# A MetaFormer layer on one core: the spectral products at full width with zero blocks instead of quarter-array products

## The chip, the core and the metric

The kernel runs on one core of a Trainium2 chip. The core has a matrix engine (TensorE, PE in the profile; its weight loads are listed as PEld), a vector engine (VectorE, DVE), a scalar engine (ScalarE, ACT), GpSimd (POOL) and a queue engine (SyncE, SP). Matmuls read SBUF and write PSUM, whose banks hold 512 float32 columns in each of 128 partitions. Each engine works through its own instructions in order; semaphores tie them together. The metric is device time in microseconds (us) of one execution; lower is better.

## The reference

One layer over x of shape (8, 128, 128, 96): a spectral mixer with a residual, then a quantised FFN with a residual.

```python
# x: (8, 128, 128, 96); MED = 192
x_pre = _soa(jnp.einsum('bhwc,mc->bhwm', _ln_c(x), w1), soa1_scale, soa1_bias)   # scale * relu(.)^2 + bias
xf = rfft2(x_pre over h, w)                                  # 128 x 65 complex, per channel
...
r = softmax over 3 of an MLP of (mean of x, mean of relu(bn(x @ sp_w)))           # (B, 3, 192)
comb = jnp.einsum('shwm,bsm->bhwm', filt, r)                 # filt: three small kernels, resized by matrices
xsp = irfft2(xf * comb)
x = x + jnp.einsum('bhwm,cm->bhwc', xsp, w2)
...
t = t + _ffn_ref(_ln_t(t), W1, b1, W2, b2)                   # fp8 (5, 2) products, 96 -> 384 -> 96
```

Both Fourier transforms are done as matrix products. All of the mixer is float32; the FFN's products are fp8.

## The kernel before

Each of the eight batches passes through three streams of operations, called `a`, `s` and `c`.

Stream `a` (32 units of four columns w): load and normalise x, project it to 192 channels plus 48 for the context (`project`, L881), rectify and square on ACT, transform along h (`transform`, L910), fold the two halves of w on DVE and store Y to DRAM. At its end the `rate_*` steps make the softmax weights `rates[b]`, one row of 2 x 192 values per partition.

Stream `s` works on groups `g` of two frequency rows h, 33 groups a batch. `load_y` brings the group's Y: 128 partitions are 64 folded positions i = 0 and 64 of i = 1, and for each there are four rows (cosine and sine of two frequencies, index `2 * cs + k`) of 192 channels. `load_t` and `weigh` (POOL) bring and scale the filter coefficients. Then, on PE,

- `along_w` (L1104) transforms along w. It cuts the 192 channels in three thirds `q` of 64. Each product is 64 rows deep (i), 64 channels wide (the half k of the output partitions) and 65 columns long; 24 a group, each on its own quarter of the array.
- `filters_of` (L1119) spreads the filter coefficients to 65 frequencies: 6 products 64 rows deep (s), 128 channels wide (two rows of one third) and 130 columns long, two halves of the array at a time.
- after `copy_sr` (ACT), `make`, `times` (DVE) and `turn_back` (POOL) have multiplied spectrum and filter into `xf`, `mix_low` and `mix` (L1200) multiply pairs `p` of groups by w2: 96 products a pair, 64 deep, 64 wide, 96 columns, accumulating over `q`, in two PSUM banks `pv`, one for each of the two frequency rows r.

`mixed` (ACT) copies half of the sums to `B`, `combine` (DVE) adds and subtracts, `invert` (L1241, L1243) transforms back along w, `inverted` (ACT) and `store_v` write V to DRAM.

Stream `c` (32 units a batch): load V and x, transform back along h (`last`, L1337), add the residual, normalise, quantise, transpose (`turn8`, L1366), first layer (`first`, L1384), cast, bias, relu on ACT and DVE, second layer (`second`, L1411), sum and store.

The order in which these operations are written to the engines is made in `in_order`: a list scheduler with a table `COST` (engine and us for each kind), a `WINDOWS` entry and an `OFFSETS` entry that give each operation its place in a priority line, and six PSUM banks to hand out. `QUARTER` names the kinds that use a divided array; a change between these and others has its own overlap in `MODES`, and `TURN` is a penalty in the priority. `WARM` names operations before which some matmuls of zeros are issued (`keep_warm`, L587). All engines then run in the written order.

Of the kernel before, what the change touches and what calls it, by code (L numbers as in the profile page):

```python
# [43 lines left out]
MED = 192  # L44
# [3 lines left out]
NS = 3  # L48
# [20 lines left out]
    "a": ((-1014.7, 224.2), (1155.2, 782.6), (913.1, 640.2), (700.4, 97.1), (81, 727.1), (986.1, 683.8), (1759.7, 398.2), (2087.9, 538.4)),  # L69
    "s": ((159.4, 351.5), (85.6, 1024.7), (720.2, 346.4), (408.4, 331.2), (-141.4, 469.9), (-95.4, 205.3), (797.8, 257), (1809.8, 30.5)),  # L70
    "c": ((1028.7, 511.2), (1109.6, 188.3), (1290.9, 349.7), (1829.7, 439.1), (2176.6, 456.9), (2490.5, 149.5), (2420.5, 484.7), (2163.8, 1143.1)),
}
OFFSETS = {
    "a_context": -69.32,
    "a_fold": 73.44,
    "a_inverse": -262.16,
    "a_load_r": 18.09,
    "a_load_x": 271.95,
    "a_load_xT": -31.56,
    "a_measure": 23.91,  # L80
    "a_project": 117.85,
    "a_put": 26.98,
    "a_rate_e": 26.43,
    "a_rate_n": 275.68,
    "a_rate_p0": -178.47,
    "a_rate_p1": 125.73,
    "a_rate_p2": -434.33,
    "a_rate_v0": -18.7,
    "a_rate_v1": 37.77,
    "a_rate_v2": 27.67,  # L90
    "a_rate_v3": 53.52,
    "a_rectify": -24.16,
    "a_rest": 88.21,
    "a_root": -155.19,
    "a_scale": 83.17,
    "a_square": 92.51,
    "a_store_r": 7.65,
    "a_store_y": -218.91,
    "a_transform": -124.2,
    "a_variance": -11.06,  # L100
    "c_accumulated": -194.42,
    "c_add_up": -37.31,
    "c_bias": -232.6,
    "c_biased": -34.16,
    "c_first": -3.46,
    "c_hidden": -99.06,
    "c_hidden_2": 18.08,
    "c_hidden_v": 120.54,
    "c_inverse": -69.89,
    "c_last": -164.57,  # L110
    "c_load_v": -0.91,
    "c_measure": 206.09,
    "c_put8": 55.17,
    "c_quantise": 161.11,
    "c_quantise_v": 272.29,
    "c_residual": -76.16,
    "c_rest": -195.99,
    "c_root": 122.09,
    "c_second": -129.32,
    "c_store": 584.16,  # L120
    "c_turn8": -377.8,
    "c_turned8": 104.13,
    "c_turned8_v": -71.45,
    "c_variance": -123.83,
    "s_alone_t": 236.02,
    "s_alone_x": 109.24,
    "s_alone_z": 223.71,
    "s_along_w": -28.38,
    "s_combine": -31.52,
    "s_copy_sr": 140.45,  # L130
    "s_filters_of": 27.98,
    "s_invert": 0.86,
    "s_inverted": -111.88,
    "s_load_t": 225.43,
    "s_load_y": 199.13,
    "s_make": 124.58,
    "s_mix": 88.61,
    "s_mix_low": -10.96,
    "s_mixed": -366.14,
    "s_store_v": 136.77,  # L140
    "s_times": -505.74,
    "s_turn_back": 28.39,
    "s_weigh": -53.57,
}
WAIT, PATIENCE, TURN = (0, 0, 0, 0.27, 0.89), (85, 74.3, 16.6, 0.273, 8.9), 454.49
# [3 lines left out]
    ('a', 0): {('project', 10, 0): 4, ('transform', 15, 2): 5, ('project', 17, 0): 4, ('project', 18, 0): 4, ('project', 19, 0): 4, ('project', 20, 0): 4, ('project', 21, 0): 4, ('project', 22, 0): 4, ('project', 23, 0): 4, ('project', 24, 0): 4, ('project', 25, 0): 4, ('project', 26, 0): 4, ('project', 27, 0): 4, ('project', 28, 0): 4, ('project', 29, 0): 4, ('project', 30, 0): 4, ('project', 31, 0): 4},  # L149
    ('a', 1): {('project', 0, 0): 4, ('transform', 0, 2): 7, ('transform', 1, 2): 4},  # L150
    ('c', 1): {('second', 12): 4, ('second', 18): 4},
    ('s', 2): {('along_w', 7): 4},
    ('a', 3): {('project', 6, 0): 3},
    ('c', 5): {('second', 21): 20, ('second', 29): 10},
    ('c', 6): {('second', 10): 12, ('second', 12): 4, ('second', 24): 14, ('second', 25): 10, ('first', 26, 0): 3, ('first', 28, 0): 4, ('first', 29, 0): 6, ('turn8', 7, 3): 10},
    ('s', 7): {('mix_low', 15): 7},
    ('c', 7): {('second', 1): 4, ('second', 5): 24, ('first', 6, 0): 8, ('second', 9): 5, ('second', 11): 9, ('last', 3, 0): 6, ('second', 13): 8, ('first', 15, 0): 4, ('second', 15): 14, ('first', 16, 0): 3, ('second', 17): 5, ('second', 19): 9, ('last', 5, 0): 16, ('second', 21): 7, ('turn8', 5, 3): 24, ('second', 23): 14, ('turn8', 6, 0): 24, ('first', 24, 0): 7, ('second', 24): 6, ('first', 25, 0): 4, ('second', 26): 8, ('second', 28): 12, ('second', 30): 10, ('turn8', 7, 3): 8, ('first', 31, 0): 4, ('second', 31): 6},
# [29 lines left out]
    "s_along_w": (PE, 0.88, 0),  # L187
    "s_filters_of": (PE, 0.94, 0),
# [4 lines left out]
    "s_weigh": (POOL, 1, 0),  # L193
    "s_mix_low": (PE, 1.22, 0),
    "s_mix": (PE, 1.22, 0),
    "s_mixed": (ACT, 0.325, 0),
    "s_combine": (DVE, 0.347, 0),
    "s_invert": (PE, 0.845, 0),
    "s_inverted": (ACT, 0.482, 0),
    "s_alone_z": (ACT, 0.75, 0),  # L200
    "s_alone_t": (DVE, 2.1, 0),
# [53 lines left out]
QUARTER = {"s_along_w", "s_filters_of", "s_mix_low", "s_mix"}  # L255
SHARED = {"a_scale", "c_biased", "a_rate_n", "a_rate_v3", "c_quantise_v", "c_hidden_v"}
INSTR = {
    "a_project": 8, "a_transform": 4, "a_rate_p0": 4, "a_rate_p1": 8, "a_rate_p2": 12, "s_along_w": 96,
    "s_filters_of": 24, "s_mix_low": 96, "s_mix": 96, "s_invert": 4, "c_last": 4, "c_turn8": 8, "c_turn32": 16,
# [33 lines left out]
def _columns(p, r):  # L293

    if p < NP - 1:
        return [(2 * p + i, k) for k in range(2) for i in range(2)]
    return [(NG - 1, 0), (NG, 0), (NG - 1, 1), (NG, 1), (NG + 1, 0)] if r == 0 else [(NG - 1, 0), (NG + 1, 0), (NG - 1, 1)]


def _constants():  # L300
# [22 lines left out]
    for p in range(NP):  # L323
        for cs in range(2):
            for r in range(2):
                for g in (2 * p, 2 * p + 1):
                    turned.append(g + 1 + 32 * r + 64 * cs if g < NG or r == 0 else 64 * (1 - cs))
    out = {
        "F1": np.concatenate([cos, sin[1:-1]])[rows].T * norm,
        "F2": np.concatenate([np.stack([half[0], -half[0]], 1), np.stack([half[1], half[1]], 1)]) * norm,  # L330
# [36 lines left out]
    rw[1, :, 1] *= -1  # L367
    out["RW"], out["SEL"] = rw.reshape(128, 2 * L), np.concatenate([sel, sel])
# [178 lines left out]
def metaformer_kernel(ctx: ExitStack, tc: tile.TileContext, a: dict, out: bass.AP):  # L547
# [68 lines left out]
    F2 = load(T_CONST, "F2", [128, 2, L])  # L616
    RW = load(T_CONST, "RW", [128, 2 * L])
    soa_bias = spread(T_CONST, "soa1_bias", 128)

    w2C = load(T_CONST, "w2C", [128, 3, C])  # L620
# [3 lines left out]
    w2N = const.tile([128, 3, C], F32, name="w2N")  # L624
# [6 lines left out]
    def projection(sp):  # L631
# [35 lines left out]
        def others():  # L667
            nc.vector.tensor_scalar(w2N, w2C, -1.0, None, ALU.mult)
            make_identity(nc, ident)
            nc.vector.tensor_copy(ident8, ident, saturate=False)  # L670
            nc.vector.memset(ones, 1.0 / (H * W))
            nc.vector.tensor_scalar(soa_bias, soa_bias, 128.0, None, ALU.mult)
# [5 lines left out]
        at(T_CONST, others, after=[(None, "soa1_bias"), (None, "w2C")])  # L678
# [155 lines left out]
    def before(b, t0, P):  # L834
# [155 lines left out]
        def rate_v2():  # L990
            hr = pa.tile([RHID, 1], F32, name="hr", tag="hr")
            hm = pa.tile([RHID, 1], F32, name="hm", tag="hm")
            kept["hrep"] = hrep = pa.tile([RHID, 128], F32, name="hrep", tag="hrep", bufs=1)
# [59 lines left out]
    def spectrum(b, t0, P):  # L1053
# [31 lines left out]
        def weigh(g):  # L1085
            p = slice(0, 128 if g <= NG else 64)
            tw = kept["tw", g] = psp.tile([128, 2 * MED], F32, name="tw", tag="tw", bufs=1)
            tb, order = kept.pop(("tb", g)), "p (k q m) -> p k q m"
            nc.gpsimd.tensor_tensor(  # L1089
                tw[p, :].rearrange("p (q k m) -> p k q m", q=3, k=2),  # L1090
                tb[p, :].rearrange(order, k=2, q=3),
                rates[b][p, :].rearrange(order, k=2, q=3),
                ALU.mult,
            )

        def along_w(g):
            halves = [bank("pz") for _ in range(2)]
            kept["pz", g] = halves
            for cs in range(2 if g <= NG else 1):
                for q in range(3):  # L1100
                    for k in range(2):
                        for i in range(2):
                            rows, c = slice(64 * i, 64 * i + 64), 2 * q + (cs if i == 0 else 1 - cs)
                            nc.tensor.matmul(  # L1104
                                halves[i][64 * k : 64 * k + 64, c * L : (c + 1) * L],
                                lhsT=kept["yt", g][rows, 2 * cs + k, 64 * q : 64 * q + 64],
                                rhs=F2[rows, cs, :],
                                start=True,
                                stop=True,
                            )  # L1110
# [26 lines left out]
        def make(g, i):  # L1137
            if ("d", g) not in kept:
                work("d", g, 2, 3, 2, L)
# [50 lines left out]
        def mix_part(p, columns):  # L1190

            for i in columns:
                for q in range(3):
                    for h in range(2):
                        for r in range(2):
                            if i >= len(_columns(p, r)):
                                continue
# [359 lines left out]
```

## Time and profile before

| | us |
|---|---|
| median of 3 runs | 2733.72 (2731.16 to 2736.47) |
| profiled execution, its own time | 2741.53 |
| its span in the profile | 2739.4 |
| PE busy | 2517.3 (92%) |
| DVE busy | 2280.6 (83%) |
| ACT busy | 2143.5 (78%) |
| POOL busy | 1691.3 (62%) |
| mean granted PE clock | 0.966 |

Busy is the time in which at least one instruction of an engine is under way. For matmuls it includes the pipeline's tail, so it overstates how full PE is. A line of the list of groups has the source line, engine, operation, output and inputs by their names in the program, the partitions x elements, the count, then the busy time, the mean length of one in ns, and the idle time before them with what ended it. One float32 product is two matmul records. HBM traffic is 407.03 MB read and 208.16 MB written, 225 GB/s over the span.

### The profile page before, as it was taken

To read this page: it belongs to the slowest core of one execution; us is meant where nothing else is said; L and a number is where in the kernel's file an instruction comes from. 1 tells how busy PE (TensorE), PEld (TensorE's weight loads), DVE (VectorE), ACT (ScalarE), POOL (GpSimd) and SP (SyncE) were. 2 spreads that over 40 slices of the span, in tenths; PEclk is the share of its full clock that TensorE was granted. 3 is DMA by queue.
4 is the path that set the end of the run, shared out by engine and by line. 5 is a ranking of instruction groups with operands and counts; after the bars stand their busy time and mean duration, and the time that the engine had idled before them with its cause. 6 is when DMAs were issued, how large, how long until landed. Compare 5 with 4: busy or idle time off the path is not lost.

```text
span 2739.4 us, 92861 instructions
## 1 busy us (share of the span) xinstructions
PE 2517.3 (92%) x37514; PEld 1803.0 (66%) x37514; DVE 2280.6 (83%) x5485; ACT 2143.5 (78%) x4332; POOL 1691.3 (62%) x2535
## 2 busy tenths in 40 slices
PE   7899999999899999899999999999999998999887
PEld 4557777767667776666776776766667665666444
DVE  5568697888898888978888988888979988889786
ACT  2356666649889798887998788988989888988866
POOL 3235454546576657756777576857766676788444
PEclk8899999999999999999999999999999999999889
DMA  8789899998867987587768988786768666575341
GB/s 227 243 262 302 255 279 291 285 272 276 260 192 244 291 258 204 186 259 240 231 198 258 289 257 260 224 243 199 234 190 250 192 201 187 153 230 157 107 137 46
DMA packets 506110, 621.22 MB, mean 227 GB/s; under 512 B 165197, under 2 KB 440038, under 8 KB 505658
## 3 DMA queue, kind: packets, MB, share of 16 engines
q1 hardware_dynamic: 417618, 464.28, 57.7%
q10 hardware_dynamic: 88064, 151.02, 15.5%
q8 instruction: 295, 4.83, 0.8%
q14 instruction: 133, 1.09, 0.1%
HBM read 407.03 MB, written 208.16 MB: 225 GB/s over the span
## 4 chain that ended last, share of the span: by engine, by line
PE 42%; ACT 17%; DVE 11%; issue 6%; DMA 4%; POOL 3%; ACTq 0%; SPq 0%; POOLq 0%; DVEq 0%
PE px L881 7%; PE py L910 6%; PE pv L1200 5%; ACT y L1391 4%; PE pf L1119 4%; PE pz L1104 4%; PE pg L1241 4%; PE pk L1337 4%; ACT h L1404 3%; ACT z L1361 3%; PE ph L1384 3%; PE po L1411 2%; DMA vin<-Vd 2%; DVE y L1395 2%; DVE t L1148 1%
## 5 line engine op out<-in xcount | busy, mean ns | idle before, releaser
L881 PE MATMUL px<-W1S,zT 97*128 97x240 f32 x2048 | 505.0, 381 | 10.6 <-DVE yst L922 5.5
L881 PEld LDWEIGHTS px<-W1S,zT 97*128 97x128 f32 x2048 | 393.1, 196 | 123.6 <-PE warm L587 10.4
L1089 POOL TENSOR_TENSOR tw<-tb,r 128x384 f32<-128x384 f32 (+1 forms) x264 | 292.1, 1106 | 259.2 <-PE pf L1119 127.6
L910 PE MATMUL py<-X,F 128*128 128x384 f32 x1024 | 435.3, 515 | 17.0 <-DVE t L1343 3.1
L1391 ACT CAST y<-ph 128x512 f16<-128x512 f32 x768 | 417.1, 604 | 25.6 <-PE ph L1384 21.6
L1404 ACT ACTIVATE h<-y 128x1536 fp8e5<-128x1536 f16 (+1 forms) x256 | 371.1, 1450 | 29.2 <-DVE y L1395 26.3
L892 ACT ACTIVATE rl<-px 128x480 f32<-128x480 f32 x512 | 292.7, 579 | 127.5 <-PE px L881 94.1
L1361 ACT ACTIVATE z<-t,ln_m,ln_r 128x96 fp8e5<-128x96 f32 x848 | 361.3, 475 | 9.1 <-POOL ln_m L826 5.6
L1395 DVE TENSOR_TENSOR y<-y,b1q 128x1536 f16<-128x1536 f16 x256 | 321.5, 1256 | 54.2 <-ACT y L1391 52.8
L906 POOL TENSOR_TENSOR sacc<-sacc,rl 128x192 f32<-128x192 f32 x248 | 175.1, 706 | 289.4 <-ACT rl L892 277.3
L1200 PE MATMUL pv<-w2C,xf 64*64 64x96 f32 x9264 | 315.6, 246 | 28.5 <-issue 25.4
L922 DVE TENSOR_TENSOR yst<-py,yb 128x384 f32<-128x384 f32 x512 | 261.7, 546 | 74.0 <-ACT rl L892 24.2
L1200 PEld LDWEIGHTS pv<-w2C,xf 64*64 64x64 f32 x9264 | 273.2, 134 | 62.7 <-issue 45.7
L1142 DVE TENSOR_TENSOR d<-pz,sr 128x390 f32<-128x390 f32 x512 | 265.2, 554 | 42.1 <-ACT sr L1135 41.7
L1148 DVE TENSOR_TENSOR t<-d,pf 128x780 f32<-128x780 f32 x256 | 245.3, 958 | 53.2 <-PE pf L1119 33.2
L1162 POOL TENSOR_TENSOR xf<-t 128x390 f32<-128x390 f32 x256 | 234.5, 916 | 66.6 <-DVE t L1148 57.6
L1119 PE MATMUL pf<-RW,tw 64*128 64x130 f32 x3120 | 252.4, 292 | 20.8 <-DVE t L1153 11.1
L1104 PE MATMUL pz<-F,yt 64*64 64x65 f32 x12480 | 250.0, 223 | 18.6 <-issue 13.2
L1384 PE MATMUL ph<-zT,W1q 96*128 96x512 fp8e5 x768 | 242.1, 387 | 23.3 <-ACT y L1391 6.5
L1426 POOL TENSOR_TENSOR o<-o,b2q 128x1536 f16<-128x1536 f16 x64 | 200.5, 3132 | 94.1 <-ACT o L1422 93.5
L1104 PEld LDWEIGHTS pz<-F,yt 64*64 64x64 f32 x12480 | 217.3, 136 | 61.4 <-issue 26.9
L1119 PEld LDWEIGHTS pf<-RW,tw 64*128 64x128 f32 x3120 | 201.3, 189 | 82.8 <-issue 30.2
(132 smaller groups left out, 5129.7 us busy)
## 6 DMA issues: line engine op xcount, KB each, us to landing
Yd<-yst ACTq DMA_DIRECT2D x256, 384.0 KB
yt<-Yd SPq DMA_DIRECT2D x248, 384.0 KB
xb<-in_xw SPq DMA_DIRECT2D x64, 768.0 KB
zT<-in_xT SPq DMA_DIRECT2D x128, 384.0 KB
rB<-Rd SPq DMA_DIRECT2D x128, 384.0 KB
tb<-T SPq DMA_DIRECT2D x256, 192.0 KB
Vd<-gst ACTq DMA_DIRECT2D x128, 384.0 KB
t<-in_x SPq DMA_DIRECT2D x64, 768.0 KB
```

The costliest lines, as they stand in the source:

```text
L881: nc.tensor.matmul(px[:, i * (MED + SCTX) : (i + 1) * (MED + SCTX)], lhsT=zTs[(b * NU // 2 + u // 2) % NZT][:, QW * (u % 2) + i0 + i, :], ...
L892: nc.scalar.activation(kept["rl", u][:, i0 : i0 + 2, :].rearrange("h w m -> h (w m)"), kept.pop(("px", u, i0)), AF.Relu)
L910: nc.tensor.matmul(py, lhsT=F1, rhs=kept["X", u][:, i0 : i0 + 2, :].rearrange("h w m -> h (w m)"), start=True, stop=True)
L1089: nc.gpsimd.tensor_tensor(tw[p, :].rearrange("p (q k m) -> p k q m", q=3, k=2), tb[p, :].rearrange(order, k=2, q=3), rates[b][p, :].rearra ...
L1104: nc.tensor.matmul(halves[i][64 * k : 64 * k + 64, c * L : (c + 1) * L], lhsT=kept["yt", g][rows, 2 * cs + k, 64 * q : 64 * q + 64], rhs=F ...
L1119: nc.tensor.matmul(pf[:, s, q * 2 * L : (q + 1) * 2 * L], lhsT=tw[p, 128 * q : 128 * q + 128], rhs=RW[p, :], start=True, stop=True,)
L1200: nc.tensor.matmul(kept["pv", p, r][half, i * C : (i + 1) * C], lhsT=kept["xf", g][rows, k, q, half], rhs=(w2N if k == 1 and h == 1 else w ...
L1361: nc.scalar.activation(z, t, AF.Identity, bias=m, scale=r, saturate=False)
L1384: nc.tensor.matmul(kept["ph", u, n], lhsT=W1q[:, n * 128 : (n + 1) * 128], rhs=kept["zT", u], start=True, stop=True)
L1391: nc.scalar.copy(kept["y", u][:, n, :], kept.pop(("ph", u, n)))
L1395: nc.vector.tensor_tensor(y, y, b1q, ALU.add)
L1404: nc.scalar.activation(h, y, AF.Relu, saturate=False)
```

## The change

The 192 channels of the two rows `k` of a group are read as one run of 384 and cut into three units of 128: the first row's channels 0 to 127, then its last 64 and the second row's first 64, then the second row's channels 64 to 191. Every product of the three lines then uses 128 rows and 128 channels, and the matrices carry zeros where a half must not contribute: F2 (transform along w) has the cosine columns in rows 0 to 63 and the sine columns in rows 64 to 127; RW (filters) has one block of 130 columns for each half; w2Z holds w2 for the shared unit, padded with zeros for each row. A group's transform has 6 products of 130 columns, its filters 4 (two of 260 columns, two of 130), a mixing part 3 for each group (192, 96 and 96 columns).

```diff
-QUARTER = {"s_along_w", "s_filters_of", "s_mix_low", "s_mix"}
+QUARTER = set()
...
-    "s_along_w": (PE, 0.88, 0),
-    "s_filters_of": (PE, 0.94, 0),
+    "s_along_w": (PE, 0.92, 0),
+    "s_filters_of": (PE, 0.84, 0),
...
-    "s_weigh": (POOL, 1, 0),
-    "s_mix_low": (PE, 1.22, 0),
-    "s_mix": (PE, 1.22, 0),
-    "s_mixed": (ACT, 0.325, 0),
-    "s_combine": (DVE, 0.347, 0),
+    "s_weigh": (POOL, 0.93, 0),
+    "s_mix_low": (PE, 0.98, 0),
+    "s_mix": (PE, 0.98, 0),
+    "s_mixed": (ACT, 0.485, 0),
+    "s_combine": (DVE, 0.552, 0),
...
+    f2 = np.zeros((128, 2, 2, L))
+    f2[:64, 0, 0], f2[64:, 0, 1], f2[:64, 1, 1], f2[64:, 1, 0] = half[0], -half[1], half[0], half[1]
...
+    signs = np.zeros((2, 64, 2, 2 * L))
+    for i in range(2):
+        signs[i, :, i] = rw[i].reshape(64, 2 * L)
+    out["RW"], out["SEL"] = signs.reshape(128, 4 * L), np.concatenate([sel, sel])
...
-            nc.gpsimd.tensor_tensor(
-                tw[p, :].rearrange("p (q k m) -> p k q m", q=3, k=2),
-                tb[p, :].rearrange(order, k=2, q=3),
-                rates[b][p, :].rearrange(order, k=2, q=3),
-                ALU.mult,
-            )
+            nc.gpsimd.tensor_tensor(tw[p, :], kept.pop(("tb", g))[p, :], rates[b][p, :], ALU.mult)
+
+        def unit(t, u):
+
+            return t.rearrange("p k m -> p (k m)")[:, 128 * u : 128 * u + 128]
 
         def along_w(g):
...
+            kept["pz", g] = [bank("pz") for _ in range(2 if g <= NG else 1)]
+            for cs in (1, 0) if g <= NG else (0,):
+                for u in range(3):
                     nc.tensor.matmul(
+                        kept["pz", g][cs][:, u * 2 * L : (u + 1) * 2 * L],
+                        lhsT=unit(kept["yt", g][:, 2 * cs : 2 * cs + 2, :], u),
+                        rhs=F2[:, cs, :],
                         start=True,
                         stop=True,
                     )
 
+        def filters_of(g):
+            pf = kept["pf", g] = psz.tile([128, 2, 512], F32, name="pf", tag="pf")
+            p = slice(0, 128 if g <= NG else 64)
+            tw = kept.pop(("tw", g))[p, :].rearrange("p (k m) -> p k m", k=2)
+            if g <= NG:
+                parts = ((0, 0, 0, 2), (1, 0, 2, 1), (1, 1, 0, 1), (2, 1, 1, 2))
+            else:
+                parts = ((0, 0, 0, 1), (1, 0, 1, 1), (2, 0, 2, 1))
+            for u, half, slot, n in parts:
+                s = 1 if (u, half) == (1, 1) else 0
+                nc.tensor.matmul(
+                    pf[:, half, slot * 2 * L : (slot + n) * 2 * L],
+                    lhsT=unit(tw, u),
+                    rhs=RW[p, s * 2 * L : (s + n) * 2 * L],
+                    start=True,
+                    stop=True,
+                )
...
-                work("d", g, 2, 3, 2, L)
+                work("d", g, 3, 2, 2 * L)
             op = ALU.subtract if i == 0 else ALU.add
-            d = kept["d", g][:, i].rearrange("p q c l -> p (q c l)")
-            nc.vector.tensor_tensor(d, kept["pz", g][0][:, : 6 * L], kept["sr", g], op)
+            a, b = (t.rearrange("p (u n) -> p u n", u=3) for t in (kept["pz", g][0][:, : 6 * L], kept["sr", g]))
+            nc.vector.tensor_tensor(kept["d", g][:, :, i, :], a, b, op)
...
+        def mix_part(p, s):
+
+            pv = kept["pv", p, s] = bank("pv")
+            for g in (2 * p, 2 * p + 1) + ((NG + 1,) if p == NP - 1 and s == 0 else ()):
+                x = kept["xf", g]
+                c0 = 2 * (g - 2 * p) - (g > NG)
+                rows = (0,) if g == NG else (0, 1)
+                nc.tensor.matmul(
+                    pv[:, c0 * C : (c0 + len(rows)) * C],
+                    lhsT=x[:, 2 + s, :],
+                    rhs=w2Z[:, rows[0] : rows[0] + len(rows), :].rearrange("m r c -> m (r c)"),
+                    start=True,
+                    stop=False,
+                )
+                for i, r in enumerate(rows):
+                    nc.tensor.matmul(
+                        pv[:, (c0 + i) * C : (c0 + i + 1) * C], lhsT=x[:, 4 * r + s, :], rhs=w2A[:, r, :], start=False, stop=r == rows[-1]
+                    )
 
         def mix_low(p):
...
+            mix_part(p, 1)
 
         def mix(p):
...
+            mix_part(p, 0)
+
+        def mixed(p):
+            v = kept["B", p] = psp.tile([128, 4 * C], F32, name="B", tag="B")
+            n = (3 if p == NP - 1 else 4) * C
+            nc.scalar.copy(v[:, :n], kept["pv", p, 1][:, :n])
...
+        def combine(p, cs):
...
+            at(t, mix_low, p, after=xf, banks=1, until=[one("mixed", p)])
+            at(t, mix, p, after=[one("mix_low", p)], banks=1, until=[done])
+            at(t + 0.0003, mixed, p, after=[one("mix_low", p)] + [one("combine", p - 2, cs) for cs in range(2)] + last)
+            for cs in range(2):
+                at(t + 0.1 * cs * P + 0.0004, combine, p, cs, after=[one("mix", p), one("mixed", p), v_free[cs]])
```

Left out above: the second mixing sums and the last group (`alone_*`) follow the same layout; `w2N`, the negated copy of w2, is gone; a small tile of the softmax steps (`hrep`) shares its buffer with another (`mx`). `mixed` copies all 384 columns of one bank at once, and `combine` runs twice a pair instead of four times. All values of `WINDOWS`, `OFFSETS`, `WAIT`, `PATIENCE` and `TURN` are others, so the written order of every engine is another. `WARM` issues 787 matmuls of zeros instead of 472. Behind the last mixing product PE has 180 first-layer products instead of 120.

## The prediction

> **What bounds the kernel now.** I read the busy shares first, then the slices, then TensorE's groups, then three stretches, then the order of single groups.
>
> ```profile
> span 2739.4 us, 92861 instructions
> PE 2517.3 (92%) x37514; PEld 1803.0 (66%) x37514; DVE 2280.6 (83%) x5485; ACT 2143.5 (78%) x4332; POOL 1691.3 (62%) x2535
> PE   7899999999899999899999999999999998999887
> PEclk8899999999999999999999999999999999999889
> ...
> L1200 PE MATMUL pv<-w2C,xf 64*64 64x96 f32 x9264 | 315.6, 246 | 28.5 <-issue 25.4
> L1119 PE MATMUL pf<-RW,tw 64*128 64x130 f32 x3120 | 252.4, 292 | 20.8 <-DVE t L1153 11.1
> L1104 PE MATMUL pz<-F,yt 64*64 64x65 f32 x12480 | 250.0, 223 | 18.6 <-issue 13.2
> ```
>
> PE is the fullest engine in nearly every slice, at a granted clock near 1, and the three lines that the change rewrites are among its largest. Each float32 product is two matmul records in the trace, two passes. A mean of 223 ns for a 65-column pass says little, because passes overlap; I need the time from the start of one group to the start of the next. That is in the order of PE's instructions (start, length, count):
>
> ```profile
> 1405.42 0.97 PE L881 MATMUL px<-W1S,zT 97*128 97x240 f32 x4
> 1406.23 0.39 PE L1366 MATMUL pz<-ident,z 128*96 128x128 fp8e5 x4
> 1406.46 0.81 PE L1384 MATMUL ph<-zT,W1q 96*128 96x512 fp8e5 x3
> 1407.11 0.97 PE L881 MATMUL px<-W1S,zT 97*128 97x240 f32 x4
> ...
> 1416.88 0.94 PE L1119 MATMUL pf<-RW,tw 64*128 64x130 f32 x12
> 1417.75 0.93 PE L1104 MATMUL pz<-F,yt 64*64 64x65 f32 x48
> 1418.50 1.20 PE L1200 MATMUL pv<-w2C,xf 64*64 64x96 f32 x48
> 1419.49 0.72 PE L1104 MATMUL pz<-F,yt 64*64 64x65 f32 x34
> ```
>
> The last line is cut by the end of the window asked for. From start to start: two 240-column products on the whole array 0.81 us, so 0.81/480 = 1.69 ns a column; the 12 passes of the filters 0.87; the 48 passes of the transform along w 0.75; the 48 of a mixing part 0.99. In the last two, four 64x64 products run at once: at 1.69 ns, 24 products of 65 columns one after the other would take 2.6 us.
>
> ```profile
> 555.23 0.93 PE L1104 MATMUL pz<-F,yt 64*64 64x65 f32 x48
> 556.09 0.91 PE L1241 MATMUL pg<-V,GL 128*128 128x384 f32 x2
> 556.84 0.65 PE L1241 MATMUL pg<-V,GM 128*128 128x288 f32 x2
> 557.33 0.36 PE L1243 MATMUL pg<-V,GL 128*128 128x96 f32 x2
> 557.52 1.41 PE L881 MATMUL px<-W1S,zT 97*128 97x240 f32 x6
> ```
>
> Here full-size products stand alone: 288 columns 0.49 us (1.70 ns a column), 96 columns 0.19 us. And 0.86 us against 0.75 for the same transform shows what leaving a divided array costs: 0.11.
>
> ```profile
> 0.00:225.00 225.00, 193.47 (x669) 115.08 (x670) 140.24 (x494) 96.72 (x174) 69.75 (x209) 0.89 0.82 248
> 225.00:2530.00 2305.00, 2156.12 (x35750) 1598.22 (x35749) 1986.13 (x4656) 1896.47 (x3869) 1526.81 (x2203) 0.98 0.77 236
> 2530.00:2740.00 210.00, 167.71 (x1099) 89.71 (x1096) 154.20 (x337) 150.32 (x292) 94.71 (x124) 0.90 0.31 98
> ```
>
> These are stretches (length, busy PE, PEld, DVE, ACT, POOL, clock, DMA share, GB/s). The three lines run only in the middle one, from 217 us (first filter) to 2523 us (last mixing).
>
> **What PE must do in the middle, before.** By the intervals above, times the counts of PE's order: px 880 products x 0.405 = 356; py 444 x 0.645 (the 384 columns at 1.68) = 286; pg 164; pk 224 x 0.645 = 144; ph 648 x 0.216 (three in 0.65) = 140; po 109; turning 48; warming matmuls 15; rest 7: 1270 us. The three lines, with their changes of the array's division inside: transform 260 full groups, 0.70 to 0.86 by their neighbours, on average 0.81: 211; filters 260 x 0.87 = 227; mixing 256 x 1.09 = 279; and about 280 entries out of whole-array work, each lengthening the product before by 0.09: 25. Together 742. So 2012 of 2305 us, 87%; the other 293 us are waits and some slower clock.
>
> **The change, part by part.** (1) Removed: the 742 us. (2) Added: whole-array products in which half of the matrix is zero. One column still costs about 1.69 ns: a 130-column product 0.222, a 260-column one 0.438, a 192-column one 0.325 us. The transform has 1560 products of 130: 346. The filters 536 of 130 and 512 of 260: 119 + 224 = 343. Mixing has 504 of 192 and 1040 of 96. For 96 columns the row L1243 gives 0.19; the passes alone would be 0.164 (1.69 x 96), and the second pass of that row, from its start to the next product, took 0.112 in the trace's records, which doubled bounds it above at 0.224. I take 0.194, the row itself: 164 + 202 = 366. Sum 1055; with the bounds 1024 to 1086. So PE gains 313 us of work.
>
> The Trainium skill ("TensorE: Matmul & The Clock Gate", section "LDWEIGHTS (loading the stationary operand)") speaks against the change: loading takes columns/1.2 ns, 107 ns for 128, whatever the row count, so a 96-column pass would wait for its weights. By it the mixing's small products would cost 1040 x 0.214 = 223 us, an estimate, for 202. Another page speaks for it ("TensorEngine Tiling (Array Packing)", "Instruction Overhead"): some 60 cycles for each matmul, 25 ns at the first page's 2.4 GHz. With 27888 passes becoming 8304 that would, as an estimate, give back 490 us and make the kernel faster; the trace disagrees, since a group of 48 passes took 0.70 us at its fastest, under 15 ns a pass.
>
> (3) Warming matmuls: 472 become 787. In the middle 68 become 216: 148 x 0.218 (the median interval in the records) = 32, and 31 more bursts, each with an entry and an exit, 10. (4) The order: on PE the FFN work left behind the last mixing product grows from 120 to 180 first-layer products, 40 to 60 units. That takes 36 us of PE out of the middle and puts it at the end. There ACT sets the pace: a unit of an earlier batch is three y casts (0.604), one h (1.450), one o (0.498), one turn (0.602) and 3.5 z (0.475), 6.0 us; the end now takes 210/40 = 5.2 us a unit. 20 units: 90 to 120, I take 110. (5) Off PE, each small: V<-pv,B and V<-B,pv 248 pairs of 0.350 and 0.343 become 120 pairs of some 0.546 (a 128x384 row, yst) and 8 smaller: DVE saves about 39 us. B copies 83 us become about 62 on ACT. POOL's weighing loses its strided order: 1.10 us, between 0.706 (128x192) and that, say 0.92 as xf's 128x390: 47 us. The d tiles are now written in three pieces; that lies between 0.55 (now) and 0.96 (the 780-element rows) and I keep 0.55: strides within one partition. None of this counts, because PE covers it: DVE has 1986 of 2305 us busy in the middle. Were PE not the bound, DVE's 39 us would come off. The constants grow by some 200 KB of DMA, in a first stretch that moves 248 GB/s: below 1 us. The mixing copy now waits for mix_low alone and holds one bank, not two: a shorter wait, hidden likewise.
>
> **Sum.** Middle: 1270 - 36 + 32 + 10 + 1055 = 2331 us of PE work. How much of its time can PE be filled? Over the middle it is 87%. Added up in the same way, the fullest 100 us stretches hold 96 and 94 us, the emptiest in the middle 75. With 16% more work against waits that other engines (DVE 86%, ACT 82% now) then meet earlier, I take 95%: 2331/0.95 = 2454. First stretch 225, unchanged (the same 144 px and 68 py). End 210 + 110 = 320. Total 2999 against the span of 2739.4. The median, 2733.7, lies 6 us under the span, so 2993: about 2995 us, 9.5% slower.
>
> **Rivals.** *The waits swallow it.* PE waits 293 us in the middle and gains about 319. If it never waited and the added units fitted into ACT's present gaps at the end: 225 + 2331 + 210 = 2766, with cheap 96s 2735; partly so, 2766 to 2890. For it: ACT is 72% busy at the end. Against: no 100 us stretch is without waits, and the FIFO order of the end leaves ACT nothing to run ahead on. 8%.
> *The waits stay in proportion.* The new order was laid out with shorter products than they are, and PE stays at 87%: 2331/0.873 = 2670, total 3215; between 3130 and 3300. For it: the middle's waits are spread over hundreds of short ones on ACT and DVE. Against: a later PE finds these done. 10%.
> *Faster.* The order's own table puts the new groups at 0.92, 0.84 and 0.98 us, 0.163 of which it counts as overlap: 0.757, 0.677, 0.817. Were that so, 260, 260 and 257 groups are 583 us, the middle 1276 + 583 = 1859, at 87.3% 2130, total 225 + 2130 + 320 = 2675. The place is the cost of a 130-column pass pair; break-even at 2739 needs 2194 x 0.873 - 1276 = 639 us for all, 0.135 us instead of 0.222. Against it: every full-size float32 row, from 96 to 384 columns, gives 1.7 ns a column or more. 4%.
> My forecast has the remaining 78%.
>
> **How the numbers follow.** The range takes the bounds of the small products (31 us each way) and 91 to 98% filling: 225 + 2331/0.98 - 31 + 320 = 2893, and 225 + 2331/0.91 + 31 + 320 = 3138; I write 2890 to 3130. It leaves out the rivals, about 2 in 10. What differs by less than 0.2%, 5 us, cannot be told from no change. Faster 0.04 (the third rival), same 0.01 (the edge of the first), slower 0.95.
>
> **What would show it.** Transform groups of 12 passes 1.33 us from start to start; filter groups 1.32; a mixing part 1.4; PE busy 96% or more in the middle, DVE and ACT lower; no 0.09 steps except around warming matmuls; an end of some 320 us. I am wrong if a transform group takes under 0.8 us, or if PE's middle is no fuller than now.

## The result, and the profile after

The changed kernel takes 3036.7 us (median of 4 runs, 3030.6 to 3043.2) against 2735.1 us for the kernel before in the same comparison: a ratio of 1.110, 95% interval 1.107 to 1.113. The profiled execution has a span of 3028.4 us.

The head of the page, and four groups of its list, of the changed kernel:

```profile
span 3028.4 us, 54180 instructions
PE 2875.0 (95%) x18245; PEld 2211.4 (73%) x18245; DVE 2257.9 (75%) x5236; ACT 2158.2 (71%) x4196; POOL 1690.5 (56%) x2535
PE   7899999999899999999999999998999999999877
PEclk8999999999999999999999999999999999999999
...
L1102 PE MATMUL pz<-F,yt 128*128 128x130 f32 x3120 | 395.2, 276 | 4.0 <-DMA yt<-Yd 2.5
L1120 PE MATMUL pf<-RW,tw 128*128 128x260 f32 (+1 forms) x2096 | 392.6, 330 | 0.6 <-POOL xf L1163 0.5
L1203 PE MATMUL pv<-w2A,xf 128*128 128x96 f32 x2048 | 298.8, 268 | 0.0
L1195 PE MATMUL pv<-w2Z,xf 128*128 128x192 f32 (+1 forms) x1040 | 263.1, 335 | 2.9 <-ACT y L1382 2.4
```

Half as many matmul records (18245 for 37514), and yet PE is busy for 358 us more, while DVE, ACT and POOL have nearly the work that they had (DVE 23 us less, ACT 15 more). The idle time ahead of the three lines has all but gone (from some 76 us to 7.5): PE now runs straight through them. In the order of PE's instructions (start, length, count):

```profile
1396.57 0.67 PE L1402 MATMUL po<-W2q,h 128*128 128x96 fp8e5 x12
1397.08 1.56 PE L1120 MATMUL pf<-RW,tw 128*128 128x260 f32 x8
1398.47 1.50 PE L1102 MATMUL pz<-F,yt 128*128 128x130 f32 x12
1399.81 0.49 PE L1195 MATMUL pv<-w2Z,xf 128*128 128x192 f32 x2
1400.14 0.58 PE L1203 MATMUL pv<-w2A,xf 128*128 128x96 f32 x4
1400.56 0.52 PE L1195 MATMUL pv<-w2Z,xf 128*128 128x192 f32 x2
1400.91 0.58 PE L1203 MATMUL pv<-w2A,xf 128*128 128x96 f32 x4
1401.33 0.60 PE L1375 MATMUL ph<-zT,W1q 96*128 96x512 fp8e5 x2
...
1403.62 1.49 PE L1120 MATMUL pf<-RW,tw 128*128 128x260 f32 x8
1404.95 1.50 PE L1102 MATMUL pz<-F,yt 128*128 128x130 f32 x12
1406.29 0.81 PE L1236 MATMUL pg<-V,GM 128*128 128x384 f32 x2
```

From start to start a transform takes 1.34 us (0.75 to 0.86 before), a filter group 1.33 in the second case shown and at the median (1.39 in the first; 0.87 before), a mixing part 1.52 (0.99 to 1.15, with its exit). The stretches, cut at the first filter and behind the last mixing product (length, busy PE, PEld, DVE, ACT, POOL, clock, DMA share, GB/s):

```profile
0.00:225.00 225.00, 188.87 (x695) 113.92 (x696) 143.43 (x502) 101.32 (x181) 77.22 (x213) 0.92 0.84 260
225.00:2727.00 2502.00, 2429.78 (x15855) 1962.74 (x15854) 1906.56 (x4265) 1804.24 (x3521) 1463.87 (x2124) 1.00 0.67 211
2727.00:3028.00 301.00, 256.38 (x1700) 134.72 (x1698) 207.96 (x470) 252.68 (x497) 149.38 (x199) 0.95 0.34 107
```

The middle is 197 us longer and the end 91. In the middle PE is busy 97% of the time, DVE 76% and ACT 72%, and PE's granted clock is 1.00 where it was 0.98. In the end, which has 20 more units of the FFN, ACT is about as full as PE, whose share holds 478 warming matmuls.

For the comparisons below I cut each run exactly at its first product of the three lines and its last, and add up PE's work between them: each pass at its undisturbed interval (2.4 ns and, for each column, 0.833 ns for float32 and half of that otherwise; at least 0.111 us where 128 float32 weight columns are loaded; divided by how many run side by side) plus 0.092 us for each change of the array's division. The two constants fit the usual intervals in the trace of before: float32 passes of 96, 240 and 384 columns stand 0.082, 0.202 and 0.322 us apart, fp8 passes of 96 and 512 columns 0.042 and 0.215. "Fill" is that work over the length of the middle.

| run | median us | middle | PE work in it | fill | end |
|---|---|---|---|---|---|
| kernel before | 2735 | 2306 | 1956 | 84.8% | 217 |
| changed kernel | 3037 | 2514 | 2359 | 93.8% | 305 |
| e6: before's products, new order | 2854 | 2329 | 1974 | 84.7% | 309 |
| e4: transform and filters back | 2889 | 2365 | 2107 | 89.1% | 304 |
| e3: transform back | 2975 | 2444 | 2238 | 91.6% | 304 |
| e1: filters back | 2969 | 2448 | 2238 | 91.4% | 306 |
| e2: transform on halves | 3120 | 2595 | 2405 | 92.7% | 306 |
| e7: fewer warming matmuls | 3041 | 2528 | 2305 | 91.2% | 304 |
| e11: narrow mixing | 3036 | 2509 | 2359 | 94.0% | 306 |
| e10: filters twice | 3377 | 2853 | 2697 | 94.5% | 304 |
| e5: changed products, old order | 3239 | 2557 | 2275 | 89.0% | 460 |
| e8: changed kernel, true costs | 3283 | 2595 | 2299 | 88.6% | 473 |
| e9: before, transforms twice | 3063 | 2629 | 2130 | 81.0% | 215 |
| e12: before, one wide product more | 2858 | 2424 | 2144 | 88.5% | 220 |

The formula comes out short for divided groups: a filter group on halves, with its exit, makes 0.76 us by it and takes 0.87 at the median; a quarter transform followed by whole-array work makes 0.77 and takes 0.86. Added up over the groups, some 50 us of work are missing in the rows of before, e6, e4, e9 and e12, some 20 in e1 and e3, 12 in e2 and none in the changed kernel. With them before's fill is 87%, as the prediction had it, and the changed kernel has some 350 us more PE work than before, not 403.

### The profile page after: what moved, and what is told of

It reads as the page before. It is cut to its first block, busy times and chain, and to the rows that moved or that the text cites. A ratio compares the mean times of both kernels' runs of the same rounds, so it can differ in the third digit from the quotient of the medians.

```text
span 3028.4 us, 54180 instructions
## 1 busy us (share of the span) xinstructions
PE 2875.0 (95%) x18245; PEld 2211.4 (73%) x18245; DVE 2257.9 (75%) x5236; ACT 2158.2 (71%) x4196; POOL 1690.5 (56%) x2535
## 5 line engine op out<-in xcount | busy, mean ns | idle before, releaser
L885 PE MATMUL px<-W1S,zT 97*128 97x240 f32 x2048 | 494.8, 374 | 25.6 <-DVE tk L729 6.7
L885 PEld LDWEIGHTS px<-W1S,zT 97*128 97x128 f32 x2048 | 380.4, 192 | 125.2 <-PE warm L592 11.4
L914 PE MATMUL py<-X,F 128*128 128x384 f32 x1024 | 426.5, 504 | 13.9 <-ACT X L903 3.9
L1102 PEld LDWEIGHTS pz<-F,yt 128*128 128x128 f32 x3120 | 383.7, 191 | 40.1 <-ACT y L1382 5.0
L1102 PE MATMUL pz<-F,yt 128*128 128x130 f32 x3120 | 395.2, 276 | 4.0 <-DMA yt<-Yd 2.5
L1120 PE MATMUL pf<-RW,tw 128*128 128x260 f32 (+1 forms) x2096 | 392.6, 330 | 0.6 <-POOL xf L1163 0.5
L1120 PEld LDWEIGHTS pf<-RW,tw 128*128 128x128 f32 x2096 | 305.1, 191 | 43.5 <-issue 2.4
L1203 PE MATMUL pv<-w2A,xf 128*128 128x96 f32 x2048 | 298.8, 268 | 0.0
L1203 PEld LDWEIGHTS pv<-w2A,xf 128*128 128x128 f32 x2048 | 295.1, 191 | 0.0
L1195 PE MATMUL pv<-w2Z,xf 128*128 128x192 f32 (+1 forms) x1040 | 263.1, 335 | 2.9 <-ACT y L1382 2.4
```

The lines of the kernel that those rows point to most:

```text
L885: nc.tensor.matmul(px[:, i * (MED + SCTX) : (i + 1) * (MED + SCTX)], lhsT=zTs[(b * NU // 2 + u // 2) % NZT][:, QW * (u % 2) + i0 + i, :], ...
L914: nc.tensor.matmul(py, lhsT=F1, rhs=kept["X", u][:, i0 : i0 + 2, :].rearrange("h w m -> h (w m)"), start=True, stop=True)
L1102: nc.tensor.matmul(kept["pz", g][cs][:, u * 2 * L : (u + 1) * 2 * L], lhsT=unit(kept["yt", g][:, 2 * cs : 2 * cs + 2, :], u), rhs=F2[:, cs ...
L1120: nc.tensor.matmul(pf[:, half, slot * 2 * L : (slot + n) * 2 * L], lhsT=unit(tw, u), rhs=RW[p, s * 2 * L : (s + n) * 2 * L], start=True, s ...
L1195: nc.tensor.matmul(pv[:, c0 * C : (c0 + len(rows)) * C], lhsT=x[:, 2 + s, :], rhs=w2Z[:, rows[0] : rows[0] + len(rows), :].rearrange("m r ...
L1203: nc.tensor.matmul(pv[:, (c0 + i) * C : (c0 + i + 1) * C], lhsT=x[:, 4 * r + s, :], rhs=w2A[:, r, :], start=False, stop=r == rows[-1])
```

## The experiments

Theory 1 is the prediction's: PE's own work sets the middle, and the wide products are more of it. Theory 2: the newly written order made the loss.

### Parts put back, in the changed kernel's order

**e1, the filters on halves of the array.**

```diff
+            if g <= NG:
+                for u, s in ((0, 0), (0, 1), (1, 0), (1, 1), (2, 0), (2, 1)):
+                    h = slice(64 * s, 64 * s + 64)
+                    nc.tensor.matmul(pf[:, s, u * 2 * L : (u + 1) * 2 * L], lhsT=unit(tw, u)[h, :], rhs=RW[h, s * 2 * L : (s + 1) * 2 * L], start=True, stop=True)
+                return
```

> The changed kernel, in its own order, with the filter products alone put back to 64 rows deep, two halves of the array at a time: 6 products of 130 columns for each of 256 groups instead of 4 over all rows. The filters land in other columns than the multiply expects, so the output is not the reference's; the work on every other engine is the same. Theory 1 (PE's own work sets the middle): a filter group falls from 1.33 to 0.87 us with its exits, less 0.09 for the entry that the product before pays: 256 x 0.37 = 95 us of PE, so 2930 to 2960 us from 3037. Theory 2 (the new written order made the loss, the products' shape did not): within 20 us of 3037.

2968.7 us, 68 less than the changed kernel. Not theory 2; the size is a little short of theory 1's. A filter group takes 0.87 us, as forecast.

**e3, the transform on quarters.**

```diff
+            if g <= NG:
+                for cs in (1, 0):
+                    for u in range(3):
+                        for h in range(2):
+                            for i in range(2):
+                                rows, blk = slice(64 * i, 64 * i + 64), cs if i == 0 else 1 - cs
+                                nc.tensor.matmul(
+                                    kept["pz", g][i][64 * h : 64 * h + 64, (2 * u + blk) * L : (2 * u + blk + 1) * L],
+                                    lhsT=unit(kept["yt", g][:, 2 * cs : 2 * cs + 2, :], u)[rows, 64 * h : 64 * h + 64],
+                                    rhs=F2[rows, cs, blk * L : (blk + 1) * L], start=True, stop=True,
+                                )
+                return
```

> As the run with half-array transforms, but 64 rows, 64 channels and 65 columns, 24 products a group on quarters of the array (output not the reference's for the same reason). Theory 1 and both views of the weight load: 0.75 to 0.86 us a group as in the kernel before, plus 0.09 on the product before, for 1.34: 256 x 0.43 = 110 us of PE, so 2920 to 2950. Theory 2: within 20 us of 3037.

2975.0 us, 62 less. Right in sign, short in size again, though a transform takes 0.86 us, as forecast.

**e4, both.**

> Transform on quarters and filters on halves together, mixing wide, the changed kernel's order (output not the reference's). Theory 1: the savings add up, some 225 us of PE (filters and transform often follow each other, which saves changes of division), with some of it lost because PE is then filled less than 94%: 2810 to 2860. If something else than PE becomes the bound on the way, the sum of the two single savings is missed by more than 60 us. Theory 2: near 3037.

2888.8 us: 148 less, where the two single savings sum to 130. They add up. But the sizes are all under what was expected because I had let too little of the saved work turn into waiting: along this row of runs with one order (e6, e4, the mean of e1 and e3, changed) PE's work rises by 133, 131 and 121 us in the table, by about 127, 107 and 97 with what the formula leaves out, and the middle by 36, 81 and 68. Of some 330 us in all, 185 come through. The mixing was not put back alone: the step from e4 to e6, 35 us of time, holds it together with the smaller operations off PE that go with it.

### The new order

**e6, the products of before under the new tables** (`WINDOWS`, `OFFSETS`, `WAIT`, `PATIENCE`, `TURN`, `WARM` of the changed kernel in the kernel before), and **e5**, the reverse.

> The kernel before, with its quarter products and costs, under the changed kernel's tables of places, offsets, waits and warming matmuls. Theory 1: the products are cheap, so most of the loss is gone: 2740 to 2860, slower than before by what the order, the 20 more units behind the last mixing product and the 315 warming matmuls cost. Theory 2: near 3037.

> The changed kernel with the tables of places, offsets, waits and warming matmuls of the kernel before (its 472 warming matmuls too), so that the scheduler places the wide products by the old priorities; the cost table stays the changed one. Theory 1: PE has the same wide products and 315 fewer warming matmuls (42 us less in the middle, a shorter end), but an order not fitted to it: 2960 to 3080. Theory 2 (the new order made the loss): below 2850.

e6: 2853.7 us, ratio 1.043 (1.039 to 1.046), within theory 1's range. Its middle is only 23 us longer than before's; its end is 92 us longer. e5: 3239.2 us, 1.184 (1.181 to 1.187), outside both expectations: the old tables make the changed kernel 202 us slower still. The last mixing products tell where the end begins. First the kernel before, the changed kernel, e6, then e5, each from its view of the mixing sums (last start behind "to"):

```profile
L1200 PE MATMUL pv<-w2C,xf x9264: 239/243/419, 242.2 to 2522.7; 64*64 64x96 f32 x198
```
```profile
L1203 PE MATMUL pv<-w2A,xf x2048: 244/275/275, 231.0 to 2722.9; 128*128 128x96 f32 x187
```
```profile
L1207 PE MATMUL pv<-w2C,xf x9264: 239/243/419, 234.1 to 2542.7; 64*64 64x96 f32 x198
```
```profile
L1196 PE MATMUL pv<-w2A,xf x2048: 244/275/422, 245.3 to 2778.2; 128*128 128x96 f32 x187
```

Behind them lie 217 us of the span before, 305 after, 309 in e6 and 460 in e5. In e5 the longer end and waits of PE on ACT are the loss. Its waits of PE, longest first (total, times, longest):

```profile
PE po L1395 <- ACT h L1388: 97.9, 63, 5.0
PE ph L1368 <- ACT zT L1364: 35.4, 33, 6.3
```

In the changed kernel the same wait for h is 14.4 us in all. So the order is worth 100 us and more either way, but it did not make this loss: with the products of before it costs 119 us, of which 92 are the end, and the wide products cost 183 us on top (2854 to 3037). That split holds for the new order: under the old tables the same products cost 504 us (2735 to 3239).

**e8, the scheduler told the true costs.**

```diff
-    "s_along_w": (PE, 0.92, 0),
-    "s_filters_of": (PE, 0.84, 0),
+    "s_along_w": (PE, 1.50, 0),
+    "s_filters_of": (PE, 1.49, 0),
...
-    "s_mix_low": (PE, 0.98, 0),
-    "s_mix": (PE, 0.98, 0),
+    "s_mix_low": (PE, 1.68, 0),
+    "s_mix": (PE, 1.68, 0),
```

> The changed kernel with its scheduler's costs of the wide products set to what the trace shows plus the 0.163 that it counts as overlap (transform 1.50, filters 1.49, mixing parts 1.68 for 0.92, 0.84, 0.98); all other tables stay. Theory 1: PE is 94% filled in the middle, so an order that knows the costs can win at most the 6%: 2960 to 3060. Rival (the wrong costs made the loss): below 2900.

3282.8 us, ratio 1.200 (1.196 to 1.204): worse than either side. As in e5 the end is the larger part of the loss: 473 us. That the priorities suit only the costs that they came with is the likely reading; no run tests it. Better costs without new priorities are no gain here, and how much a refitted order would win stays open.

**e7, fewer warming matmuls.**

```diff
-        n = WARM.get(op.key[0], {}).get(op.key[1:], 0)
+        n = WARM.get(op.key[0], {}).get(op.key[1:], 0) if op.key[0] in (None, ("a", 0), ("c", 6), ("c", 7)) else 0
```

> The changed kernel with the warming matmuls kept only for the first batch's projection and the last two batches' FFN (and the setup). Theory 1: where PE is the bound they are plain work; those left out and lying in the full middle are 60 to 100, 0.218 us each and 0.3 a burst: 15 to 35 us faster, granted clock in the middle still 0.99 or more. Rival: they hold the clock, and without them the time is the same or longer.

3041.1 us (3037.4 to 3044.2), no gain. None are left in the middle (216 fewer than in the changed kernel, more than the expectation counted), 54 us of PE work less, and still the median is 4 us longer, which is within the scatter. (The middle of the profiled execution is 14 us longer, but that one is the slowest of its four, and the changed kernel's the fastest.) The stretch from 1725 to 2225 us, with the columns of the stretches above, first of the changed kernel, then of e7:

```profile
1725.00:2225.00 500.00, 474.37 (x3095) 368.63 (x3094) 380.79 (x908) 380.55 (x743) 304.53 (x450) 0.99 0.65 206
```
```profile
1725.00:2225.00 500.00, 456.80 (x2962) 362.17 (x2961) 378.99 (x904) 376.92 (x731) 296.91 (x445) 0.96 0.63 200
```

Without them the granted clock falls from 0.99 to 0.96 there and from 1.00 to 0.98 over the middle. All four executions agree: over the whole span the clock is 0.972 or 0.973, for 0.980 to 0.986 in the changed kernel. PE's waits on ACT's h go from 14.4 to 30.5 us, its idle time in the middle from 72 to 109. So the work saved comes back as wider gaps and a slower clock; how much each takes was not separated.

### What sets the price of a wide product

**e2, the transform on halves of the array**, with half the columns a pass and the same 128 weight columns (as e3, with 128 channels for 64 and no loop over h).

> The changed kernel, in its own order, with the transform along w alone as products of 64 rows, 128 channels and 65 columns, 12 for each of 256 groups, two halves of the array at a time; parts land in the other bank, so the output is not the reference's. A pass has half the columns of before and as many weight columns. If columns alone count: 12 pairs of passes x 0.057 + 0.14 for entry and exit = 0.82 us a group for 1.34, some 125 us less: about 2920. If a load of 128 weight columns sets a floor of 0.112 us under each pass: 12 x 0.112 + 0.14 = 1.48, some 35 us more than the changed kernel: 3050 to 3080.

3119.9 us, 83 more than the changed kernel. In the order of PE's instructions:

```profile
1410.06 1.56 PE L1106 MATMUL pz<-F,yt 64*128 64x65 f32 x24
1411.54 0.91 PE L1342 MATMUL pk<-vin,GK 128*128 128x384 f32 x2
```

1.48 us for 12 pairs of passes, as the weight floor said, not 0.82. The kernel lost more than the 37 us of the group itself. A part is paid by the neighbours for the changes of division: a filter group's median rose from 1.326 to 1.388, some 16 us over 256 groups, and the mixing parts rose too. By the table, with the 12 us that the formula leaves out, PE's work grew by some 60 us; the rest of the middle's 81 is waiting, which no run takes apart.

**e11, narrower mixing products.**

```diff
-                        pv[:, (c0 + i) * C : (c0 + i + 1) * C], lhsT=x[:, 4 * r + s, :], rhs=w2A[:, r, :], start=False, stop=r == rows[-1]
+                        pv[:, (c0 + i) * C : (c0 + i) * C + 64], lhsT=x[:, 4 * r + s, :], rhs=w2A[:, r, :64], start=False, stop=r == rows[-1]
```

> The changed kernel with the 1024 mixing products of 96 columns cut to 64 (a third of their output columns is left out, so the output is not the reference's). A pass is 0.082 us for 96 columns and 0.056 for 64. If the passes follow their columns, a mixing part falls from 1.51 by 8 x 0.027 = 0.21 us, 55 us of PE in all, some 30 us of time. If the weight load of 128 columns is the floor, 0.112 a pass, a part stays at 1.45 to 1.51 and the time within 15 us of the changed kernel.

3036.5 us, the changed kernel's time, though a third of the columns of 1024 products is gone.

```profile
1401.77 0.49 PE L1195 MATMUL pv<-w2Z,xf 128*128 128x192 f32 x2
1402.10 0.55 PE L1203 MATMUL pv<-w2A,xf 128*128 128x64 f32 x4
1402.49 0.55 PE L1195 MATMUL pv<-w2Z,xf 128*128 128x192 f32 x2
1402.87 0.55 PE L1203 MATMUL pv<-w2A,xf 128*128 128x64 f32 x4
1403.26 0.60 PE L1375 MATMUL ph<-zT,W1q 96*128 96x512 fp8e5 x2
```

A part takes 1.49 us for 1.52. One in four of these passes, the one behind a wide pass, follows its columns (0.082 us with 96, 0.056 with 64); the other three stay 0.111 apart with either. e2 and e3 point the same way: a pass of 65 columns takes 0.11 us where 128 weight columns are loaded, and about 0.064 where 64 are. So under 130 columns the load of 128 float32 weight columns, about 0.11 us a pass, is what counts for most passes; that it is the load, and not something else that comes with 128 weight columns, is the reading of these runs.

### How much added PE work shows

**e10, each filter product twice in the changed kernel** (`parts + parts`), and **e9, each transform twice in the kernel before** (`for cs in (0, 1, 0, 1)`).

> The changed kernel with each filter product of 256 groups issued twice into the same place (the output stays the reference's): 256 x 1.32 = 338 us more PE work. Theory 1: at 94% fill little is left to absorb, 96 to 98% is the end: the middle goes from 2514 to between 2750 and 2810, 240 to 300 us more in all. Rival (half is absorbed here too): 130 to 200 us more.

> The kernel before, in its own order, with each transform along w of 256 groups issued twice into the same place (the output stays the reference's): 256 x 0.70 = 179 us more PE work in the middle and nothing else. Theory 1, with the curve of the runs so far (in one order, 133 us more work at a fill of 85% cost 36 us, the next 131 cost 81): a third to a half comes through, 50 to 90 us more than the kernel before. Rival (each us of PE is a us of time, fill stays): 170 to 210 us more.

e10: 3377.1 us, 340 more for 338 us of work, more than expected. In the changed kernel nothing of added work is absorbed any longer: a microsecond of PE is a microsecond of time, and the middle less its work stays at 155 us. e9: 3062.5 us, 323 us more (than 2739.1 in its own comparison) for 174 of work, far outside both expectations. The waits of PE for nothing but its own instructions ("issue"; total, times, longest), first before, then e9:

```profile
PE pv L1200 <- issue: 33.8, 22, 3.4
PE pz L1104 <- issue: 13.2, 7, 3.0
PE pf L1119 <- issue: 0.6, 2, 0.5
```
```profile
PE pz L1104 <- issue: 79.7, 48, 5.0
PE pv L1200 <- issue: 77.7, 44, 4.6
PE pf L1119 <- issue: 8.8, 7, 3.9
```

And the row of the queue that brings instructions (packets, MB, share), in the same order and then of the changed kernel:

```profile
q8 instruction: 295, 4.83, 0.8%
```
```profile
q8 instruction: 391, 6.41, 0.9%
```
```profile
q8 instruction: 145, 2.38, 0.3%
```

24576 more instructions, 96 more packets: 256 instructions a packet. Gaps within groups of the three lines (over 0.26 us between passes, over 0.5 in the filters) sum to 61 us before, 190 in e9 and 2 in the changed kernel. The traces show where they stand. Counted through PE's matmuls, weight loads and semaphore events in the order of their starts, all 31 waits on issue of the three lines in before, and all 99 in e9, come at the 194th or 195th of a block of 256 instructions, and each ends 1.0 to 1.7 us behind the landing of a packet of this queue; only 8% of the passes of these lines start so. Two such packets start 3.3 us apart at the least, while 128 passes (a block holds as many weight loads) at 15 ns take 1.9.

**e12, the same PE time in few instructions.**

```diff
+            if g <= NG:
+                nc.tensor.matmul(
+                    halves[0][:, : 2 * MED], lhsT=GL, rhs=kept["yt", g][:, 0:2, :].rearrange("p k m -> p (k m)"), start=True, stop=True
+                )
```

> The kernel before with the same added PE time as the run with doubled transforms, but in few instructions: one full-size product of 384 columns (0.645 us, and 0 to 0.2 for entry and exit) ahead of each of 256 transforms, into a place that the transform then overwrites (the output stays the reference's). 165 to 215 us more PE work; 2 matmul records a group more instead of 48. If the doubled transforms cost 323 us because the many short instructions outran their delivery (the waits on issue in the three lines rose), those waits stay where they were before, near 61 us, and the time rises by 60 to 170 us. If each us of PE work in this order costs as much whatever its instructions, it rises by 300 us or more.

2857.9 us, 125 more for 188 of work. The waits on issue did not rise, they fell by half:

```profile
PE pv L1204 <- issue: 11.5, 12, 3.3
PE pz L1108 <- issue: 9.8, 7, 2.5
PE pf L1123 <- issue: 4.1, 3, 2.0
```

With nearly the same PE work added, many short instructions cost 323 us and a few long ones 125. The gaps account for 157 of these 198 us (190 in e9, 33 in e12). The granted clock in the middle differs too, 0.97 in e9 and 1.00 in e12; whether that follows from the gaps was not tested. e3 and e4, with quarter transforms but wide mixing, have no wait on issue in the three lines. So PE runs out of instructions where short passes follow each other for long enough: the place of the waits shows it, though no run changed how the instructions are brought.

## Why the prediction was right, point by point

- *A column costs 1.69 ns whatever the array holds.* Right: transform 1.340 us (1.33 forecast), filters 1.326 (1.32).
- *Mixing.* Right in kind, mis-sized: 1.515 us a part for some 1.43. I took the 96-column product at 0.194 from one row. In a part three in four of these passes stand 0.111 apart and one in four 0.082, and one in four of the 192-column passes takes 0.191 for 0.162. That is 0.09 x 256 = 23 us. By "TensorE: Matmul & The Clock Gate", section "LDWEIGHTS (loading the stationary operand)", which I weighed and did not follow, 128 columns take 128/1.2 = 107 ns, an estimate, and that was nearer: e2 and e11 measure 0.11 us a pass.
- *The end.* 110 more was forecast; the stretches give 91, and e6 has 92 with the old products. So it is the order, as said, not the products. The price was too high: ACT is busy 253 us there for 60 units, 4.2 a unit, where the sum had 6.0.
- *Warming matmuls.* The 42 us in the sum were wrong: e7 shows that without them no time is won.
- *The filling, 95%.* Measured 93.8%. It was a choice, not worked out from a run, and that it came so near was partly luck: e5 and e8, with nearly the same PE work, reach 89%, and e5's 3239 us lies in the range of the rival of waits in proportion.
- *Left out.* I had not priced that the quarter groups lose 61 us before (54 in e6) to gaps between their own instructions, which the wide ones do not. That, a granted clock in the middle of 1.00 for 0.98, and shorter waits on the other engines are, as far as the traces show, most of why some 330 us more work from e6 to the changed kernel cost 185 us of time.
- *Off PE.* Nothing there shows in the time, as said, though no run varied it alone. POOL's weighing took 1.09 us for 1.10, not the 0.92 that I expected without the strided order, and DVE saved 23 us, not 39.

The total came out 1.4% over the forecast: the middle from 225 us took 2502 for 2454 (mixing 23 more and a lower fill, against no cost of warming), the end 301 for 320. So errors of both signs stand in the sum.

The rivals: *the waits swallow it* fails, since more than half came through; *in proportion* fails in this order, whose fill rose from 87% to 93.8%; *faster* fails on the 1.34 us.

## What to carry to other kernels

Count columns, not instructions: a matrix padded with zeros costs what a full one costs (1.7 ns a float32 column here), and dividing the array pays when a product's depth and width are half of it (0.86 us for 1.34 in e3). Two things bound that: a load of 128 float32 weight columns sets a floor of 0.11 us under most passes, so that halves with 65 columns lost (e2), and long rows of very short instructions run out of instructions. In a kernel whose order is written ahead, products under the other kernel's order lost 119 us (e6) and 202 (e5), about as much as the wide products themselves (183).

## What was not expected of the hardware

- Quarter-array groups start a pass every 15 ns and then, at some boundaries of 256 instructions, stop until the next ones come: 1.5 us at the median of 99 waits in e9. 12288 more of such passes, on 27888, made three times the gaps (61 to 190 us); one long product ahead of each transform halved them (33).
- A change of the array's division costs 0.09 us each time, on the instruction ahead of it: in before a 512-column fp8 product takes 0.308 us for 0.215 when a divided group follows, a 240-column float32 pass 0.295 for 0.202.
- Warming matmuls that look like waste in a full engine were free: taking 216 out of the middle lowered the granted clock from 0.99 to 0.96 in one stretch and won nothing.
